# Layer 0 of a four-layer image stack in strips of 16 rows: q and k in one pass with a gathered block transform, v in a second pass

## The chip, the core and the metric

The kernel runs on one core of one Trainium2 chip. A core has TensorE (PE in the profile: matrix products, with PEld for its weight loads), VectorE (DVE), ScalarE (ACT), GpSimd (POOL) and SyncE (SP), which issues DMAs; ACT and POOL issue DMAs too. The five work from queues of their own, each in order, and wait for each other by semaphores. Products go to PSUM (8 banks of 2 KB in each of 128 partitions)[...]. All data are 32-bit floats; a product of such data is issued as two instructions. The metric is the device time of one execution in microseconds (us), the median of several runs.

## What is computed

The input x is (4, 48, 256, 256): 4 images of 48 channels. Four layers follow each other, each of the form x = x + f(groupnorm(x)) with 16 groups. Layer 0, which the change rewrites:

```python
hidden = conv1x1(gn(x), w_hidden) + b_hidden            # 48 -> 288 channels
qkv = depthwise3x3(hidden, w_dw, padding='SAME') + b_dw  # per channel
q, k, v = split(qkv, 3)                                  # 96 channels each
out = irfft2(rfft2(q in 8x8 blocks) * rfft2(k in 8x8 blocks))
normed = (out - mean_c) / sqrt(var_c + 1e-5) * gamma + beta   # over the 96 channels
x = x + conv1x1(v * normed, w_out) + b_out               # 96 -> 48 channels
```

Layers 1 and 2 go the other way about: a 1x1 product to 288 channels, each 8x8 block transformed, multiplied by a mask and transformed back, then a depthwise 3x3 product, gelu of one half times the other half, and a 1x1 product to 48. Layer 3 is a gate from block maxima and variances. Only the order of some steps of layers 1 and 2 is touched, and layer 3 not at all.

## The kernel before

Layer 0 (`layer0`, L227) works in bands of 8 rows, 32 per image, 128 in all. Positions lie on the partitions after the first product. In three steps that are staggered by one band each (the loop at L429):

- `conv_step` (L262) loads 10 rows of x, normalises them (L284), and makes shifted copies with DMAs on SP (L288 to L292), so that the 1x1 and the 3x3 products are a single product: its weights are the products of both (L248, L251). For each half row of 128 positions 4 products of 288 columns add up in PSUM: one of 58 rows (L308) and three of 128 rows (L315). ACT copies q and k out (L320), DVE v (L321).
- `attend_step` (L324) takes four half rows at a time: three products of 384 columns with transform matrices (L335), DVE's two products (L343), two products back (L353), and then mean and variance over the channels (L364 to L374; the power -0.5 is on POOL), scale, gamma, beta on POOL (L375 to L380), and times v on DVE (L381).
- `out_step` (L384) turns the result with products by the unit matrix (L392), multiplies by the output weights (L405), adds x (L407), takes statistics for the next layer (L192) and stores.

The statistics of x itself, for the normalisation of layer 0, come from `stats_step` (L256): all rows of image 0 before its first band, those of image b+1 beside the bands of image b.

Layers 1 and 2 (`layers12`, L442) work in strips of 16 rows, 16 per image, 64 per layer. For strip n, positions of a 8x8 block lie on 64 partitions, for 288 channels in three thirds m: `forward` (L522: normalise, L531; turn, L544; transform, L556), `mix` (L566: 1x1 product, L578, and the mask on DVE, L583), `inverse` (L590: transform back, L604, and ACT's and DVE's copies into z, L612), then halo copies of neighbouring positions within z by DMA, three on SP (L616 to L618) and three on POOL (L619 to L621, the last stores what the strip below needs). `gate` (L628) does the depthwise product: for each channel a 100x64 matrix of taps (built by `build_taps`, L494) times the 64 blocks of z (L640), gelu on ACT (L647), product on DVE (L648). `project` (L671) turns (L655, L658), multiplies (L682) and adds to `res` (L687). `store` (L693) takes the statistics of the 8 rows of `res` (L699) and stores them (L703); `load_res` (L663, L669) then loads the next residual. `bottom` (L707) does the last row of an image. The loop at L752 sets the order: inverse(n,0), gate(n-1,2), mix(n,1), finish(n-1), inverse(n,1), mix(n,2), gate(n,0), forward(n+1), inverse(n,2), mix(n+1,0), gate(n,1).

The functions give the order of the work only roughly: a scheduler sorts the instructions of each engine by when it expects their operands, so an instruction can stand ahead of another that the text has first. Tiles come from pools with a number of buffers; a new tile waits for the last reader of the tile whose buffer it gets. PSUM has 8 tiles of one bank in layer 0 and 4 tiles of two banks in layers 1 and 2.

Of the kernel before, what the change touches and what calls it, by code (L numbers as in the profile page):

```python
# [10 lines left out]
F32 = mybir.dt.float32  # L11
AF = mybir.ActivationFunctionType
ALU = mybir.AluOpType
# [58 lines left out]
def _fft_matrices():  # L72

    rows, real = _frequencies()  # L80
    pr, pc = np.divmod(np.arange(P * P), P)
    names = ("fq", "fr", "fi", "g1", "g2")
    m = {k: np.zeros((128, 128), np.float64) for k in names}
    for row, ((ky, kx), imag) in enumerate(rows):
        angle = 2 * np.pi * ((ky * pr + kx * pc) % P) / P
        cos, sin = np.cos(angle), np.sin(angle)
        weight = (1.0 if (ky, kx) in real else 2.0) / (P * P)
        own = (ky, kx) in real
        for h in (0, 64):
            at = slice(h, h + 64)  # L90
            m["fr"][at, h + row] = cos
            m["fi"][at, h + row] = 0.0 if own else -sin
            m["fq"][at, h + row] = -sin if imag else cos
            m["g1"][h + row, at] = -weight * sin if imag else weight * cos
            m["g2"][h + row, at] = -weight * cos if imag else (0.0 if own else -weight * sin)
    order = np.array([P * r + c for r, c in _order()])
    gz = m["g1"][:, np.concatenate([order, 64 + order])]
    return np.stack([m[k] for k in names] + [gz], 1).astype(np.float32)
# [36 lines left out]
def _ones_rows():  # L135

    padded = np.pad(np.ones((W, W), np.float32), 1)
    out = np.ones((3, 10, P, W), np.float32)
    for n, h0 in enumerate((0, P, W - P)):
        for t in range(9):  # L140
            dy, dx = divmod(t, 3)
            out[n, t] = padded[h0 + dy : h0 + dy + P, dx : dx + W]
    return out
# [16 lines left out]
def conv_stack_kernel(ctx: ExitStack, tc: tile.TileContext, t: dict):  # L160
# [24 lines left out]
    def new_stats(pool, key, bufs):  # L185
        tag = f"stats_{key.rstrip('0123456789')}"
        return pool.tile([C, W // 2, 6], F32, tag=tag, name=f"stats_{key}", bufs=bufs)

    def add_stats(stats, row, rows):

        for n in range(0, rows.shape[1], 2):
            nc.vector.bn_stats(stats[:, (row + n) // 2, :], rows[:, n : n + 2, :])  # L192

# [19 lines left out]
    def over_block(v):  # L213

        return v.rearrange("p (r j c) -> p r j c", r=1, c=1).to_broadcast([C, P, 16, P])

# [10 lines left out]
    def layer0():  # L227
        with ExitStack() as st:
            wp = st.enter_context(tc.tile_pool(name="l0w", bufs=1))
            sb = st.enter_context(tc.tile_pool(name="l0", bufs=2))  # L230
            psum = st.enter_context(tc.tile_pool(name="l0ps", bufs=8, space=PSUM))

            def weight(name, shape):
                dst = wp.tile(shape, F32, tag=name, name=name)
                nc.scalar.dma_start(dst, t[name])
                return dst
# [3 lines left out]
            wh1, w1 = weight("l0_wh1", [128, C6]), weight("l0_wd1", [128, 3, C6])  # L240

            wh2 = wp.tile([122, C6], F32, tag="l0_wh2", name="l0_wh2")
            w2 = wp.tile([122, C6], F32, tag="l0_wd2", name="l0_wd2")
            for p0 in (0, 64):
                nc.scalar.dma_start(wh2[p0 : p0 + 58], t["l0_wh2"])
                nc.scalar.dma_start(w2[p0 : p0 + 58], t["l0_wd2"])
            for k in range(3):
                nc.vector.tensor_tensor(w1[:, k, :], w1[:, k, :], wh1, ALU.mult)  # L248
            for p0 in (0, 64):
                at = slice(p0, p0 + 58)  # L250
                nc.vector.tensor_tensor(w2[at], w2[at], wh2[at], ALU.mult)  # L251
            fft = weight("fft", [128, 6, 128])
            gamma, beta = weight("l0_gamma", [128, C2]), weight("l0_beta", [128, C2])
            w_out, b_out = weight("l0_w_out", [C2, C]), weight("l0_b_out", [C, 1])

            def stats_step(b, band, stats):  # L256
                for row in range(band * P, band * P + P, 4):
                    xt = sb.tile([C, 4, W], F32, tag="xstat", name=f"xstat_{b}_{row}")
                    nc.scalar.dma_start(xt, x_in[b, :, row : row + 4, :])
                    add_stats(stats, row, xt)  # L260

            def conv_step(b, band, mean, rstd):  # L262

                key = f"{b}_{band}"
                lo, hi = max(band * P - 1, 0), min(band * P + P + 1, W)
                at = lo - (band * P - 1)
                n = hi - lo
                xt = sb.tile([C, P + 2, W], F32, tag="x0", name=f"x0_{key}", bufs=4)
                nc.sync.dma_start(xt[:, at : at + n, :], x_in[b, :, lo:hi, :])
                k1 = sb.tile([128, P + 2, W + 2], F32, tag="k1", name=f"k1_{key}")  # L270

                k2 = sb.tile([122, P // 2, W], F32, tag="k2", name=f"k2_{key}")
                kind = 0 if band == 0 else 2 if band == NBAND - 1 else 1
                for i in range(2):
                    nc.sync.dma_start(
                        k2[64 * i + 48 : 64 * i + 58], t["ones"][kind, :, 4 * i : 4 * i + 4]
                    )
                nc.gpsimd.memset(k1[:C, :, 0:1], 0.0)
                nc.gpsimd.memset(k1[:C, :, W + 1 : W + 2], 0.0)
                if band == 0:  # L280
                    nc.gpsimd.memset(k1[:C, 0, :], 0.0)
                if band == NBAND - 1:
                    nc.gpsimd.memset(k1[:C, P + 1, :], 0.0)
                nc.vector.tensor_scalar(  # L284
                    k1[:C, at : at + n, 1 : W + 1], xt[:, at : at + n, :], mean[:C], rstd[:C],
                    ALU.subtract, ALU.mult,
                )
                nc.sync.dma_start(k1[48:96, 0:P, :], k1[0:48, 1 : P + 1, :])  # L288
                nc.sync.dma_start(k1[96:128, 0:P, :], k1[0:32, 2 : P + 2, :])
                for k in range(3):  # L290
                    for i in range(2):
                        nc.sync.dma_start(  # L292
                            k2[64 * i + 16 * k : 64 * i + 16 * k + 16],
                            k1[32:48, 2 + 4 * i : 6 + 4 * i, k : k + W],
                        )
                qk = sb.tile([128, 2 * P, 2 * C2], F32, tag="qk", name=f"qk_{key}")
                v = sb.tile([128, 2 * P, C2], F32, tag="v", name=f"v_{key}", bufs=3)
                for r in range(P // 2):


                    gs = [(i, h) for h in range(2) for i in range(2)]
                    ps = {
                        (i, h): psum.tile([128, 512], F32, tag="ps", name=f"qkv_ps_{key}_{r}_{i}_{h}")
                        for i, h in gs
                    }
                    for i, h in gs:
                        at = slice(64 * i, 64 * i + 58)
                        nc.tensor.matmul(  # L308
                            ps[i, h][:, :C6], k2[at, r, 128 * h : 128 * h + 128], w2[at],
                            start=True, stop=False,  # L310
                        )
                    for i, h in gs:
                        row, w0 = r + 4 * i, 128 * h
                        for k in range(3):
                            nc.tensor.matmul(  # L315
                                ps[i, h][:, :C6], k1[:, row, w0 + k : w0 + k + 128], w1[:, k, :],
                                start=False, stop=(k == 2),
                            )
                        g = 2 * row + h
                        nc.scalar.copy(qk[:, g, :], ps[i, h][:, : 2 * C2])  # L320
                        nc.vector.tensor_copy(v[:, g, :], ps[i, h][:, 2 * C2 : C6])  # L321
                return xt, qk, v

            def attend_step(b, band, qk, v):  # L324

                key = f"{b}_{band}"
                o = sb.tile([128, 2 * P, C2], F32, tag="o", name=f"o_{key}")

                def products(s):
                    f = [  # L330
                        psum.tile([128, 512], F32, tag="ps", name=f"f_{key}_{s}_{n}")[:, : 4 * C2]
                        for n in range(3)
                    ]
                    for n, c0 in enumerate((0, C2, C2)):
# [637 lines left out]
```

## Time and profile before

| | us |
|---|---|
| median of 3 runs | 17339.73 |
| lowest and highest | 17327.48, 17381.77 |
| the profiled execution: its time | 17300.25 |
| its span, first to last instruction | 17298.5 |
| layer 0 (0 to the last product of its last band) | 6802 |
| layers 1 and 2 (to 16252) | 9446 |
| layer 3 | 1047 |

The page lists busy time by engine, then the span in 40 slices (a digit is the busy share in tenths; PEclk is the clock that was granted to TensorE), DMA queues, the chain that ended last, and groups of instructions by line: count, busy time, mean time of one, the idle time before them and what ended it. Busy time of a group counts overlapping instructions once, so busy time by count can be less than the mean of one. In the answers by order of time each line has its start, its length, engine, line, operation, output and inputs, shapes and count, and in brackets the idle time before it and what ended it. The chain that ended last covers only the end of layer 3 here, so it doesn't help for layer 0.

### The profile page before, as it was taken

What the parts mean: (1) busy time and instruction counts of PE and PEld (TensorE: products, weight loads), DVE (VectorE), ACT (ScalarE), POOL (GpSimd) and SP (SyncE); (2) the same over time, 40 slices, a digit from 0 to 9 for tenths busy, and PEclk for the clock granted to TensorE, in tenths of its full rate; (3) what the DMA queues carried; (4) which work ended last, traced back from release to release, by engine and by line L of the source; (5) the groups of instructions that cost most, each with busy time, mean ns of one, the idle gap of its engine ahead of it and who ended that gap; (6) DMA issues with size and microseconds to landing.
All of it is one profiled execution on the core that took longest, in us unless ns stands there. A gap on an engine that the chain in (4) does not pass through costs nothing. (4 is left out here: it accounts for less than half of the span.)

```text
span 17298.5 us, 384653 instructions
## 1 busy us (share of the span) xinstructions
PE 14947.9 (86%) x170196; PEld 10981.8 (63%) x170196; DVE 8709.8 (50%) x13299; ACT 5013.2 (29%) x7570; POOL 3388.3 (20%) x3280
## 2 busy tenths in 40 slices
PE   5999899989989998999999999999999999999400
PEld 3566566656656665777777777777777777777400
DVE  6544544444444444554554545545545545455576
ACT  1222122222222222333333333333333333333222
POOL 0222222222222222111111111111111111111245
PEclk9999999999999998998998989989989989899655
DMA  4222222222222221433433333423433433343467
GB/s 99 58 43 40 63 41 42 40 38 41 43 39 39 41 43 31 87 84 79 86 84 78 84 77 83 87 62 85 88 75 83 88 77 84 79 86 83 84 139 167
DMA packets 276304, 1231.56 MB, mean 71 GB/s; under 512 B 96507, under 2 KB 146757, under 8 KB 163797
## 3 DMA queue, kind: packets, MB, share of 16 engines
q1 hardware_dynamic: 153120, 651.58, 19.1%
q0 software_dynamic: 94720, 452.75, 11.8%
q10 hardware_dynamic: 26804, 102.62, 2.3%
q8 instruction: 1345, 22.04, 0.5%
q14 instruction: 315, 2.57, 0.1%
HBM read 528.04 MB, written 281.54 MB: 47 GB/s over the span
## 5 line engine op out<-in xcount | busy, mean ns | idle before, releaser
L315 PE MATMUL qkv_ps<-l_wd,k 128*128 128x288 f32 x12288 | 3131.2, 412 | 0.0
L315 PEld LDWEIGHTS qkv_ps<-l_wd,k 128*128 128x128 f32 x12288 | 2300.0, 190 | 797.3 <-issue 202.1
L640 PE MATMUL c_ps_False<-z,d 100*64 100x64 f32 x73728 | 2550.1, 235 | 274.8 <-DVE z L612 96.4
L640 PEld LDWEIGHTS c_ps_False<-z,d 100*64 100x64 f32 x73728 | 2497.3, 152 | 423.9 <-DVE z L612 223.4
L612 DVE COPY z<-z_ps 64x1024 f32<-64x1024 f32 x1152 | 1349.0, 1223 | 1387.9 <-ACT z L612 1372.9
L578 PE MATMUL y_ps<-w_in,f 48*128 48x96 f32 x24576 | 1748.8, 298 | 194.2 <-DVE z L612 183.5
L578 PEld LDWEIGHTS y_ps<-w_in,f 48*128 48x128 f32 x24576 | 1617.0, 207 | 471.2 <-DVE z L612 243.8
L647 ACT ACTIVATE g<-c_ps_False 128x512 f32<-128x512 f32 x1152 | 687.9, 597 | 3329.7 <-PE c_ps_False L640 3327.7
L320 ACT COPY qk<-qkv_ps 128x192 f32<-128x192 f32 x2048 | 647.3, 318 | 3327.9 <-PE qkv_ps L315 3045.0
L583 DVE TENSOR_TENSOR yf<-y_ps,mask 128x384 f32<-128x384 f32 x3072 | 1464.6, 547 | 38.5 <-PE y_ps L578 30.0
L648 DVE TENSOR_TENSOR g<-g,c_ps_False 128x512 f32<-128x512 f32 x1152 | 788.4, 687 | 1296.5 <-ACT g L647 1285.3
L658 ACT COPY gt<-gt_ps 72x1024 f32<-72x1024 f32 x1024 | 970.7, 1030 | 1008.8 <-PE gt_ps L655 1008.8
L612 ACT COPY z<-z_ps 64x1024 f32<-64x1024 f32 x1152 | 1087.5, 1008 | 580.7 <-PE z_ps L604 563.0
L321 DVE COPY v<-qkv_ps 128x96 f32<-128x96 f32 x2048 | 473.1, 249 | 1319.9 <-ACT qk L320 1319.8
L604 PE MATMUL z_ps<-yf,dft 64*64 64x512 f32 x9216 | 1120.4, 611 | 7.9 <-DVE yf L583 4.1
L687 DVE TENSOR_TENSOR res<-xo_ps,res 112x1024 f32<-112x1024 f32 x256 | 313.8, 1226 | 1550.9 <-PE xo_ps L682 1544.9
L335 PE MATMUL f<-qk,fft 128*128 128x384 f32 x3072 | 1069.7, 491 | 17.9 <-DVE v L321 17.9
L655 PEld LDWEIGHTS gt_ps<-ident,g 128*72 128x72 f32 x8192 | 904.0, 161 | 127.2 <-issue 111.6
L655 PE MATMUL gt_ps<-ident,g 128*72 128x128 f32 x8192 | 962.1, 276 | 8.6 <-issue 6.6
L682 PE MATMUL xo_ps<-gt,w_out 72*64 72x512 f32 x4096 | 935.4, 598 | 0.0
L619 POOL DMA_DIRECT2D z<-z x384 | 200.9, 523 | 3715.7 <-DVE z L612 3713.7
L343 DVE TENSOR_TENSOR pr<-fq,f 128x384 f32<-128x384 f32 x1024 | 562.6, 553 | 690.9 <-PE f L335 672.0
(135 smaller groups left out, 16261.8 us busy)
## 6 DMA issues: line engine op xcount, KB each, us to landing
z<-z SPq DMA_DIRECT2D x1152, 203.9 KB
xf<-x POOLq DMA_DIRECT2D x256, 384.0 KB, 7.7
x<-x SPq DMA_DIRECT2D x256, 384.0 KB
res<-x POOLq DMA_DIRECT2D x248, 384.0 KB, 6.0
x<-res POOLq DMA_DIRECT2D x248, 384.0 KB, 5.0
carry<-z POOLq DMA_DIRECT2D x384, 204.0 KB, 9.1
z<-carry SPq DMA_DIRECT2D x384, 203.9 KB
x<-in_x SPq DMA_DIRECT2D x120, 480.0 KB
```

What stands on the lines that cost most here:

```text
L315: nc.tensor.matmul(ps[i, h][:, :C6], k1[:, row, w0 + k : w0 + k + 128], w1[:, k, :], start=False, stop=(k == 2),)
L335: nc.tensor.matmul(f[n], fft[:, n, :], qk[:, 4 * s : 4 * s + 4, c0 : c0 + C2], start=True, stop=True,)
L578: nc.tensor.matmul(ps[:, i, 96 * j : 96 * j + 96], f[at, 4 * h + j, :], third(w_in)[at], start=True, stop=True,)
L583: nc.vector.tensor_tensor(y[:, :, 8 * h + i : 8 * h + 8 : 2].rearrange("p (v c) j -> p v c j", v=2), ps[:, i, 0:384].rearrange("p (j v c) ...
L604: nc.tensor.matmul(ps[64 * v : 64 * v + 64, p0 // 64, :], dft[p0 : p0 + 64, 1, p0 : p0 + 64], y[p0 : p0 + 64, c0 : c0 + 16, :].rearrange(" ...
L612: copy[v](z[0:64, :, c0 : c0 + 16, 1 : NP + 1], ps[64 * v : 64 * v + 64].rearrange("p u (c j) -> p u c j", j=NP),)
L640: nc.tensor.matmul(ps[p0 : p0 + 64, v, f0 : f0 + nj], d[rows, HID * v + 48 * m + c, :], z[rows, us, 48 * v + c, 1 : NP + 1], start=True, s ...
L647: nc.scalar.activation(to, of[:, 0], AF.Gelu)
L648: nc.vector.tensor_tensor(to, to, of[:, 1], ALU.mult)
L655: nc.tensor.transpose(ps[:72, k // 4, 128 * (k % 4) : 128 * (k % 4) + 128], g[:, :, j + k], ident)
L658: nc.scalar.copy(gt.rearrange("p q u o -> p (q u o)"), ps[:72].rearrange("p k f -> p (k f)"))
L682: nc.tensor.matmul(ps[64 * i : 64 * i + 64, k, :], w_out[:, p, :], gts[k][i][:, :, p, :], start=(p == 0), stop=(p == 1),)
```

## The change

Layer 0 is rewritten on the pattern of layers 1 and 2, in two passes over all images. Both use `conv_pass` (L277 of the changed kernel), which works in 64 strips of 16 rows and one step for the last rows of all images. A tile z holds one third (96 channels) of hidden: partitions are 64 positions of a patch of 4 rows and 16 columns, then the halo and a row of ones for the bias; free are 4 patch rows, 96 channels, 16 patch columns and two of padding.

- `mixed(n)`: loads and normalises 16 rows, does the 1x1 product for each third with 49 rows (48 channels and a row of ones) and 96 columns, copies into z with ACT and DVE, and fills the halo: on SP three loads of what the strip above stored, and three copies within z; on POOL two copies within z and one store for the strip below.
- `depthwise(n)`: for each channel a 109x64 matrix of taps times 64 columns of z, 32 products to a PSUM tile of two banks, copied by ACT.
- Pass A has thirds q and k. `attend` gathers the 8x8 blocks from their four patches in the transform: for every quarter of the partitions (32 rows) four products add up, of 94 rows of output (64 frequencies and 30 sums of real and imaginary parts) and 384 columns whose elements lie 4 floats apart. ACT copies q's, DVE multiplies by k's in place (three products in place of four per complex frequency), one product of 94 rows goes back, and then the normalisation over channels on tiles twice as wide. The result goes to DRAM (`kept`).
- Pass B has v. `times_v` places it in the same order with products of 32 rows and 64 columns of weights, and multiplies the loaded result by it; `project`, one strip later, turns, multiplies by the output weights, adds x, takes statistics row by row and stores.
- Statistics of x (`stats_rows`) take two rows of both image halves at a time in three tiles.
- In layers 1 and 2 the statistics leave `store` for `add_stats`, which with `load_res` makes `settle`; `gate(n,0)` and then `settle(n-1)` come ahead of `mix(n,2)`.

The diff, cut to its core (constants, weights, and the removed functions of layer 0 are left out):

```diff
+        def conv_pass(name, c_first, thirds, coefs_of, after):
...
+            nz = 2
+            zs = [wp.tile([128, 4, 96, BW], F32, tag=f"z{i}", name=f"z_{name}_{i}") for i in range(nz)]
...
+            def above(zf, n, third):
...
+                lender = lambda src, u: (
+                    nc.sync.dma_start(zf[ABOVE, u, here], src[:, here]),
+                    nc.sync.dma_start(zf[ABOVE_L, u, here], src[15:32:16, to_left]),
+                    nc.sync.dma_start(zf[ABOVE_R, u, here], src[0:32:16, to_right]),
+                )
...
+            def mixed(n):
...
+                for third in range(thirds):
...
+                    above(zf, n, third)
+                    if b is None:
+                        continue
+                    c0 = c_first + 96 * third
+                    for g in range(4):
+                        ps = ps2(f"h_ps_{key(n)}_{third}_{g}")
+                        for j in range(4):
+                            for h in range(2):
+                                at = slice(64 * h, 64 * h + C + 1)
+                                nc.tensor.matmul(
+                                    ps[:, h, 96 * j : 96 * j + 96],
+                                    xn[at, 4 * g + j].rearrange("p r c -> p (r c)"),
+                                    w1[at, c0 : c0 + 96], start=True, stop=True,
+                                )
...
+                    nc.sync.dma_start(zf[ON_LEFT, :, here], zf[COL15, :, to_left])
+                    nc.sync.dma_start(zf[ON_RIGHT, :, here], zf[COL0, :, to_right])
+                    nc.sync.dma_start(zf[ABOVE, 1:4, here], zf[ROWS23, 0:3, here])
+                    nc.gpsimd.dma_start(zf[ABOVE_L, 1:4, here], zf[RIGHT23, 0:3, to_left])
+                    nc.gpsimd.dma_start(zf[ABOVE_R, 1:4, here], zf[LEFT23, 0:3, to_right])
+                    to = lowest[b] if s == S - 1 else carry[(n + 1) % 2]
+                    nc.gpsimd.dma_start(to[:, third, :], zf[ROWS23, 3, :])
...
+            def depthwise(n, zt):
...
+                                nc.tensor.matmul(
+                                    ps[64 * h : 64 * h + 64, k // 8, 64 * (k % 8) : 64 * (k % 8) + 64],
+                                    d[:, 96 * third + c, :], z[0:K, :, c, 1 : NJ + 1],
+                                    start=True, stop=True,
+                                )
+                        nc.scalar.copy(
+                            to[:, 16 * q : 16 * q + 16, :].rearrange("p c j -> p (c j)"),
+                            ps.rearrange("p k f -> p (k f)"),
+                        )
...
+            for n in range(N + after.lag):
+                if n < N:
+                    zt[n] = mixed(n)
+                    if n + 1 < N:
+                        load(n + 1)
+                    after.beside(n)
+                if n >= 1 and n - 1 in convolved:
+                    after.first(n - 1, convolved.pop(n - 1))
+                if after.lag > 1 and 2 <= n:
+                    after.second(n - 2)
+                if n < N:
+                    convolved[n] = depthwise(n, zt.pop(n))
...
+        def by_patch(n, what, s, ch, put):
+            for j in range(4):
+                for h, p, at in quarters:
+                    v = s[at, 24 * ch : 24 * ch + 24, :].rearrange("p c (u j) -> p c u j", j=4)
+                    put(j, h, p, at, v[:, :, :, j])
...
+            def attend(n, convolved):
...
+                    def put(j, h, p, at, moving):
+                        nc.tensor.matmul(
+                            ps[h][0:94, p, 0:384], forward[at, r, j, :], moving,
+                            start=(j == 0), stop=(j == 3),
+                        )
...
+                for ch in range(2):
+                    fs = queries(ch)
+                    keys(ch, fs)
+                    inverse(ch, fs)
...
+                nc.gpsimd.tensor_tensor(var, var, half, ALU.pow)
+                nc.gpsimd.tensor_tensor(o, o, over(var), ALU.mult)
...
+                nc.gpsimd.tensor_tensor(o, o, by_c(gamma), ALU.mult)
+                nc.gpsimd.tensor_tensor(o, o, by_c(beta), ALU.add)
+                nc.sync.dma_start(kept[n], o)
...
+            def times_v(n, convolved):
+                w = sb.tile([128, 2, C2, 16], F32, tag="w", name=f"w_{n}", bufs=3)
+                nc.sync.dma_start(w, kept[n])
...
+                            nc.tensor.matmul(
+                                ps[h][64 * r : 64 * r + 64, p, 0:384], place[at, r, j, :], moving,
+                                start=(j == 0), stop=(j == 3),
+                            )
...
         def store(n):
             layer, b, s = steps[n]
-            if s == 0:
-                stats[0] = wp.tile([HC, P * S, 6], F32, tag="stats_b", name=f"stats_{key(n)}")
-            for r in range(P):
-
-                nc.vector.bn_stats(stats[0][:, P * s + r, :], res[:, r, :])
...
+        def settle(n):
+            add_stats(n)
             if n + 1 < len(steps):
                 load_res(n + 1)
...
             inverse(n, 1)
+            gate(n, 0)
+            if late and s > 0:
+                settle(n - 1)
             mix(n, 2)
-            gate(n, 0)
```

## The prediction

> **What bounds the kernel now.** I read the page's busy shares and slices first, then the busy times by stage, then TensorE's order of time in one band of layer 0 and in one strip of layers 1 and 2.
>
> ```profile
> PE 14947.9 (86%) x170196; PEld 10981.8 (63%) x170196; DVE 8709.8 (50%) x13299; ACT 5013.2 (29%) x7570; POOL 3388.3 (20%) x3280
> ...
> PE   5999899989989998999999999999999999999400
> ...
> PEclk9999999999999998998998989989989989899655
> ```
>
> ```profile
> 0.00:6806.00 6806.00, 6207.64 (x24604) 3951.61 (x24604) 3242.42 (x5810) 1471.08 (x3457) 1711.70 (x922) 0.98 0.23 46
> 6806.00:16252.00 9446.00, 8725.76 (x145576) 7027.64 (x145576) 4682.66 (x7092) 3291.43 (x3977) 1161.93 (x2237) 0.90 0.38 81
> ```
>
> Columns of the second: stretch, length, busy PE, weight loads, DVE, ACT, POOL, granted clock, DMA share, GB/s. Layer 0 takes 6806 us with PE busy 91%, layers 1 and 2 take 9446 us with 92%, but at a clock of 0.90. Both are TensorE's.
>
> ```profile
> 6551.27 1.24 PE L308 MATMUL qkv_ps<-l_wd,k 58*128 58x288 f32 x8
> 6552.44 6.09 PE L315 MATMUL qkv_ps<-l_wd,k 128*128 128x288 f32 x24
> ...
> 6579.93 4.03 PE L335 MATMUL f<-qk,fft 128*128 128x384 f32 x12
> ...
> 6600.59 1.24 PE L308 MATMUL qkv_ps<-l_wd,k 58*128 58x288 f32 x8
> ```
>
> One band costs 49.3 us (6600.59 - 6551.27), almost all of it products that follow each other. A full-array instruction of 384 columns costs 322 ns (12 from 6579.93 to the next group at 6583.80).
>
> ```profile
> 10046.63 2.71 DVE L699 BATCH_NORM_STATS2 stats<-res 112x6 f32<-112x256 f32 x8
> ...
> 10050.65 4.93 PE L578 MATMUL y_ps<-w_in,f 48*128 48x96 f32 x48 [1.53 <-DVE z L612]
> ...
> 10055.51 8.51 PE L640 MATMUL c_ps_False<-z,d 100*64 100x64 f32 x192
> ```
>
> ```profile
> 10048.00:10052.00 4.00, 2.47 (x38) 2.31 (x34) 3.97 (x8) 1.24 (x2) 0.47 (x1) 0.91 0.79 188
> 10052.00:10056.00 4.00, 4.00 (x44) 3.83 (x43) 3.97 (x8) 0.00 (x0) 2.11 (x5) 0.50 0.89 174
> ```
>
> A strip of layers 1 and 2 takes 68.2 us. The statistics on DVE hold up its z copies, PE waits 1.53 us, and then its clock is halved for about 10 us: L578 takes 103 ns an instruction instead of 61, L640 8.5 us instead of 5.82. The same drop stands 68 us later, and again around 12040, 12108, 14020 and 14088.
>
> **What the skill says.** "TensorEngine Tiling (Array Packing)", Tiling Modes: products of at most 32 rows can run as four row tiles at once. "TensorE: Matmul & The Clock Gate", Part 3, gives 3.07x as measured for four row tiles at 512 columns. The trace agrees for 2x2 tiles: L604, 64 rows by 64 columns, costs 117 ns for 512 columns (24 in 2.81 us), against 322 x 512/384 = 429 ns for a full array, 3.7x. The same page, Part 1, has the halved clock after idle; here 1.5 us of idle sufficed. "SBUF — State Buffer", Door 1: The DMA port swizzle, says that SBUF is read in lines of 16 bytes and that each access to a new line pays a penalty. No row of before shows a moving operand of that kind.
>
> **The change, pass A (q and k), per strip of 16 rows, full clock.**
> - 1x1 product: 64 matmuls = 128 instructions. L578 has their form (64 in 3.9 us, 61 ns): 7.8 us. Their evacuation (8 copies of 768 columns each on ACT, 0.80 as L548, and on DVE, 0.95 by L612's slope) keeps pace.
> - Depthwise: 192 matmuls = 384 instructions like L640 (192 in 5.82): 11.7 us.
> - Gathering DFT: 128 matmuls = 256 instructions, 32 rows, 384 columns. Four at once would be 322/4 = 81 ns, by the page's 3.07 it is 105, two at once 161. Their moving operand steps 4 floats, a new line each time. I take 95: 24.3 us.
> - Inverse: 32 instructions of 384 columns in two column tiles, 171 ns (L682's 228 x 384/512): 5.5 us. Twice PE waits about 1 us for DVE's last product: 2 us.
> - Sum on PE: 51.3 us. ACT (25 us) and DVE (32 us, with 2x L364, L366 and L372) lie under it.
>
> But a second chain decides. From the end of one strip's inverse: evacuation 0.8, mean 3.5, subtract 3.5, squares and sums 5 make 13 us. Then POOL: power 5.4 (2x L374's 2.93, rounded down for its fixed part), times rstd 5.5, gamma and beta 6.9 each (2x L375, L379, L380), 24.7. The store of this o stands on SP ahead of the next strip's halo copies, and POOL's own halo copies stand behind the POOL work. What must then move: 1.57 MB of o and 0.79 MB of x at 238 GB/s (188 at share 0.79), 2.4 MB of halo at 165 (99 at share 0.60, 10012 to 10016): 24 us, and 2 to land. So the second third of the depthwise two attends later can't begin before T+64. Behind it follow 5.8 + 7.8 + 31.8 to the end of that attend: two periods = 109.4, one 54.7. PE then waits about 3.4 us in a strip, which by the drop above costs another 5 us of halved clock on this chain: 57 us. Without the wait 50, with DMA and POOL half as slow again 65.
> 65 x 57 = 3705.
>
> **Pass B (v), per strip.** 1x1 3.9; depthwise 5.8; placing 128 instructions of 32x64 tiles: 42 ns with eight at once, 85 with four; I take 55, 7.0 us; 64 transposing instructions at 130 ns (L392: 8 in 1.04), 8.3; output product 16 at 228, 3.7. Sum 28.7. DVE has 17 us, ACT 10, POOL 5. DMA has 5.4 MB, 24 us at the rates above, with slack of some 17 us in each strip because o is loaded a strip ahead. For bubbles and a halved clock I add 4.3 (the 4.9 us drop of before in most strips): 33. Range 29.5 to 38. 65 x 33 = 2145.
>
> **Once.** Statistics of image 0: before, 165 us with two tiles in flight; three now: 110. Depthwise matrices 128 instructions, 41 us (L502's 61.7 x 192/288). The statistics of images 1 to 3 stand in DVE's queue within the first few strips, 330 us against 5 x 57: 60 more. Zeroing for the last rows 30, end of A and start of B 110, two strips' tail of B 40. Sum 390.
>
> Layer 0: 3705 + 2145 + 390 = 6240 against 6806: -566.
>
> **Layers 1 and 2.** In the changed kernel's order on DVE the statistics lie between the z copies (5, copy, 2, copy, 1, copy), and on PE the 192 depthwise instructions follow the inverse directly, the mask product after them. Each z copy is then in time: the 1.53 us wait and the 4.9 us of halved clock go. What is late next is xn: it stands on DVE behind the 8 mask products, and the cover it had on PE (the 5.85 us of L640) now lies ahead. PE ends the mask product at +12.5 us from the inverse's start, xn's first half is ready at +15.2: a new wait of 2.7 us, ahead of products as thin as those where the clock fell. From inverse to end of forward: 26.4 us before; 23.0 with no drop, 27.6 if the clock falls there (L544 and L556 at the slow rate, +4.6). I take -1.1 us, near the middle; the ends are -3.4 and +1.2. Times 120 strips: -130 (-410 to +145). On POOL's queue the res load moves behind that strip's three halo issues (0.5 us each), which no longer wait with it for the store to land (3.6 us before 10051.53); its data is wanted 40 us later, so I cost this at nothing; without that cover it would be its 6.0 us to landing.
>
> **Sum.** 17298 - 566 - 130 = 16602 us of span; outside the span lie 1.8 us (17300.25), and the median of the runs is 39 above that: **16640**.
>
> **Rivals.**
> 1. *Row tiles don't overlap by four, or the 16-byte step halves the read (slower; 0.20).* At 161 ns the DFT takes 41.2 us: PE 68.2 us per strip, which hides the POOL chain. Pass A +11.2 x 65 = 730; placing at 85 ns, +250. 17,620. It decides from about 150 ns an instruction, where 700 us are gone. For it: no such product in the trace; against: L604's 3.7x.
> 2. *No stall and no drop (faster, 0.13).* A 50, B 29.5, layers 1 and 2 at -3.4: -455 - 230 - 280, 15,680. For it: the depthwise rows recover; against: 1.5 us sufficed for a drop.
> 3. *The POOL and SP chain is half as slow again (0.17).* A 65, B 35: +520 + 130: 17,290, about the old time, of which a fifth lies slower than 0.3% and a fifth within.
> The likeliest case, 0.50, has 16,200 to 17,050.
>
> **Chances.** A measurement of this kernel tells 0.3%, some 50 us. Slower: 0.19 of rival 1 and 0.03 of rival 3, 0.22; within: 0.01 and 0.04, 0.05; faster 0.73. The range 15,900 to 17,550 leaves out a good half of rival 1 and of rival 2, 0.2 in all.
>
> **What would show it.** Period of pass A near 57 us with PE waiting for a halo DMA between the two thirds of the depthwise; DFT instructions at 80 to 105 ns (150 or more is rival 1); period of pass B near 33; in layers 1 and 2 no wait at the mask product behind z copies but one at xp for xn, and a strip of 65 to 69.5 us. Wrong it would be if DVE or ACT lines ended PE's longest waits in either pass, or if the first strips took over 400 us.

## The result, and the profile after

| | before | after |
|---|---|---|
| median of 4 runs | 17,354.97 us | 18,428.32 us |
| ratio, 95% interval | | 1.062 (1.0599 to 1.0641) |
| profiled execution, span | 17,298.5 us | 18,418.5 us |
| layer 0 | 6806 us | 7570 us |
| layers 1 and 2 | 9446 us | 9805 us |

The change is slower, by 6.2%, where I had forecast 4% faster. Both halves of the forecast failed: layer 0 lost 764 us instead of gaining 566, and layers 1 and 2 lost 359 instead of gaining 130.

The page of the changed kernel gives busy times, TensorE (PE) in 40 slices, and the clock granted to it.

```profile
PE 15806.6 (86%) x225764; PEld 11181.0 (61%) x225764; DVE 9257.5 (50%) x10792; ACT 5900.6 (32%) x6669; POOL 4020.5 (22%) x3765
...
PE   5999999999979999899898998999989989989600
...
PEclk8889999989989999888888998997989888889755
```

The same by stage: pass A, pass B, layers 1 and 2 (columns as in the prediction).

```profile
136.00:5325.00 5189.00, 4835.32 (x51619) 2627.46 (x51622) 2676.80 (x1738) 1632.00 (x1798) 1881.01 (x769) 0.89 0.31 73
5461.00:7570.00 2109.00, 1951.93 (x28018) 1257.02 (x28017) 1028.39 (x1421) 695.43 (x711) 363.84 (x581) 0.95 0.73 163
7570.00:17375.00 9805.00, 8890.29 (x145586) 7214.75 (x145586) 4676.30 (x7111) 3296.37 (x3977) 1169.60 (x2248) 0.88 0.37 78
```

PE is busy 93% of pass A: for the most part it isn't waiting, its work takes longer than I gave it. The pass takes 5189 us against 3705; pass B takes 2109 against 2145. One strip of pass A, PE in order of time:

```profile
2799.92 11.05 PE L487 MATMUL qf<-s_qk,l_fft 32*94 32x384 f32 x64
2810.78 11.01 PE L487 MATMUL kf<-s_qk,l_fft 32*94 32x384 f32 x64
2821.72 0.86 PE L514 MATMUL o_ps<-qf,l_fft 94*64 94x384 f32 x2
...
2825.53 11.41 PE L400 MATMUL c_ps_qk<-z_qk,d_qk 109*64 109x64 f32 x380
2836.87 1.14 PE L368 MATMUL h_ps_qk<-l_w,xn_qk 49*128 49x96 f32 x16
2839.69 12.24 PE L368 MATMUL h_ps_qk<-l_w,xn_qk 49*128 49x96 f32 x112 [1.69 <-ACT s_qk L405]
```

64 instructions of the DFT take 10.86 us (2810.78 - 2799.92): 170 ns each, where I took 95 and gave 161 as the worst. The 1x1 product (L368) waits 1.69 us for ACT and then needs 109 ns an instruction (12.24 / 112) instead of 61. Both engines around that wait, another strip:

```profile
3064.58 3.36 DVE L534 TENSOR_TENSOR o<-o,mu 128x3072 f32<-128x3072 f32 x1
...
3068.03 2.86 ACT L538 ACTIVATE sq<-o 128x1536 f32<-128x1536 f32 x2 [3.53 <-DVE o L534]
...
3070.80 2.82 ACT L405 COPY s_qk<-c_ps_qk 128x1024 f32<-128x1024 f32 x3
...
3071.84 6.51 PE L368 MATMUL h_ps_qk<-l_w,xn_qk 49*128 49x96 f32 x58 [1.70 <-ACT s_qk L405]
```

ACT's squares stand ahead of the last three copies of the depthwise result and wait for DVE's subtraction. The copies come late, and with them the PSUM tiles that the 1x1 product needs. Behind the wait the granted clock is 0.50 from 3072 to 3088.

In pass B, turning (L631) and placing (L593):

```profile
6505.70 1.99 PE L631 MATMUL t_ps<-ident,w 128*96 128x128 f32 x16
...
6524.12 11.06 PE L593 MATMUL v_ps<-s_v,l_fft 32*64 32x384 f32 x128
```

Placing takes 86 ns an instruction, where I took 55. In layers 1 and 2, from one `inverse` to the end of the next `forward`:

```profile
12022.16 2.81 PE L835 MATMUL z_ps<-yf,dft 64*64 64x512 f32 x24
12024.90 5.82 PE L871 MATMUL c_ps_False<-z,d 100*64 100x64 f32 x192
12030.65 3.81 PE L809 MATMUL y_ps<-w_in,f 48*128 48x96 f32 x64
12037.19 0.40 PE L775 MATMUL xp_ps<-ident,xn 48*64 48x48 f32 x4 [2.73 <-DVE xn L762]
12038.48 6.92 PE L775 MATMUL xp_ps<-ident,xn 48*64 48x48 f32 x124 [0.89 <-DVE xn L762]
12045.33 5.54 PE L787 MATMUL f_ps<-dft,xp 128*128 128x128 f32 x32
```

The wait behind the z copies at L809 is gone, the forecast wait for xn is there with 2.73 us (2.7 forecast), and the clock falls behind it, to 0.50 from 12039 to 12048: L787 takes 171 ns an instruction (12050.80 - 12045.33 for 32), against 117 in k4 below, which has no wait there. The stretch takes 28.6 us (26.4 before). Other strips are alike: from 8000 to 16000 us the products on xn (L775) take 302 ns on the mean, against 227 before (L544), and PE waits 368 us for xn, about 3.5 us a strip.

### The profile page after: what moved, and what is told of

It is laid out like the page before. It is cut to its first block, busy times and chain, and to the rows that moved or that the text cites. A ratio compares the mean times of both kernels' runs of the same rounds, so it can differ in the third digit from the quotient of the medians.

```text
span 18418.5 us, 494130 instructions
## 1 busy us (share of the span) xinstructions
PE 15806.6 (86%) x225764; PEld 11181.0 (61%) x225764; DVE 9257.5 (50%) x10792; ACT 5900.6 (32%) x6669; POOL 4020.5 (22%) x3765
## 5 line engine op out<-in xcount | busy, mean ns | idle before, releaser
L871 PEld LDWEIGHTS c_ps_False<-z,d 100*64 100x64 f32 x73728 | 2292.2, 142 | 495.0 <-DVE z L843 246.1
L809 PE MATMUL y_ps<-w_in,f 48*128 48x96 f32 x24576 | 1512.5, 276 | 5.2 <-issue 4.5
L809 PEld LDWEIGHTS y_ps<-w_in,f 48*128 48x128 f32 x24576 | 1425.0, 188 | 150.4 <-ACT z L843 103.1
L487 PE MATMUL kf<-s_qk,l_fft 32*94 32x384 f32 x8320 | 1483.8, 850 | 33.0 <-ACT qf L500 33.0
L487 PE MATMUL qf<-s_qk,l_fft 32*94 32x384 f32 x8320 | 1489.9, 855 | 11.0 <-ACT s_qk L405 6.2
L507 DVE TENSOR_TENSOR qf<-qf,kf 94x768 f32<-94x768 f32 x520 | 473.7, 946 | 1970.0 <-PE kf L487 1966.3
L775 PE MATMUL xp_ps<-ident,xn 48*64 48x48 f32 x16384 | 964.4, 302 | 446.5 <-DVE xn L762 446.5
L775 PEld LDWEIGHTS xp_ps<-ident,xn 48*64 48x64 f32 x16384 | 929.7, 215 | 482.3 <-issue 363.3
L487 PEld LDWEIGHTS kf<-s_qk,l_fft 32*94 32x94 f32 x8320 | 489.6, 177 | 983.7 <-issue 917.5
L542 POOL TENSOR_TENSOR var<-var,neg_half 128x32 f32<-128x32 f32 x65 | 354.4, 5453 | 3206.1 <-DVE var L540 3206.1
L487 PEld LDWEIGHTS qf<-s_qk,l_fft 32*94 32x94 f32 x8320 | 463.5, 190 | 893.6 <-issue 838.3
## 6 DMA issues: line engine op xcount, KB each, us to landing
xf<-x POOLq DMA_DIRECT2D x256, 384.0 KB, 11.4
```

What stands on the lines that cost most here:

```text
L487: nc.tensor.matmul(ps[h][0:94, p, 0:384], forward[at, r, j, :], moving, start=(j == 0), stop=(j == 3),)
L507: nc.vector.tensor_tensor(f[:, h], f[:, h], ps[0:94, :, 0:384], ALU.mult)
L775: nc.tensor.matmul(ps[p0 : p0 + 64, j // 8, 64 * (j % 8) : 64 * (j % 8) + C], xn[at, 16 * h + j].rearrange("p r c -> p (r c)"), ident[at, ...
L809: nc.tensor.matmul(ps[:, i, 96 * j : 96 * j + 96], f[at, 4 * h + j, :], third(w_in)[at], start=True, stop=True,)
L871: nc.tensor.matmul(ps[p0 : p0 + 64, v, f0 : f0 + nj], d[rows, HID * v + 48 * m + c, :], z[rows, us, 48 * v + c, 1 : NP + 1], start=True, s ...
```

## The experiments

Theory after the result: (1) the DFT and the placing run at half rate because their moving operand steps 4 floats, while four row tiles do overlap; (2) layers 1 and 2 lose by the wait for xn and the halved clock behind it; (3) pass A loses some 7 us a strip because ACT's squares stand ahead of its copies. Main rival of (1): only two row tiles overlap, whatever the layout. The chips of the later runs were up to 0.5% slower (before: 17,417 to 17,446 us), so kernels are compared by their ratio to before on the same chip.

| kernel | ratio to before (95%) | strip of A | pass A | pass B | layers 1, 2 |
|---|---|---|---|---|---|
| changed kernel | 1.062 (1.0599 to 1.0641) | 78.9 | 5237 | 2087 | 9659 |
| k1_contiguous | 1.0109 (1.0092 to 1.0127) | 64.3 | 4426 | 2108 | 9643 |
| k2_read_only | 1.0104 (1.0089 to 1.0119) | | 4422 | 2112 | 9657 |
| k3_order_before | 1.0455 (1.043 to 1.0481) | | 5238 | 2076 | 9464 |
| k4_xn_ahead | 1.0144 (1.0106 to 1.0182) | | 5235 | 2089 | 8991 |
| k5_raw_squares | 1.0516 (1.0494 to 1.0537) | 77.1 | 5132 | 2106 | 9652 |
| k7_contig_squares | 0.9935 (0.9918 to 0.9951) | 60.0 | 4119 | 2103 | 9640 |
| k8_contig_halo_sp | 0.989 (0.9874 to 0.9906) | 58.1 | 4000 | 2118 | 9693 |
| k6_all | 0.9491 (0.9469 to 0.9513) | 60.0 | 4103 | 2101 | 8881 |
| k11_best | 0.9324 (0.9297 to 0.9351) | 56.4 | 3934 | 1986 | 8866 |
| k9_before_new_order | 1.0126 (1.0102 to 1.0149) | | | | 9641 |
| k12_before_again | 0.998 (one run) | | | | 9405 |
| k10_steps | 1.030 (one run) | 70.4 | | | |

Stages in us: pass A from its first 1x1 product to the last inverse, pass B from its first 1x1 product to the last placing, layers 1 and 2 from the first product on xn to the last output product. These cuts leave out set-up and ends, so they differ from the windows above. A strip of A is the mean over the 1800 us from 2000 to 3800; the number of strips in them is that of the DFT instructions divided by 256 (changed kernel: 5842, so 22.8 strips).

**k1_contiguous** and **k2_read_only.**

```diff
-    to[:, 16*q : 16*q+16, :].rearrange("p c j -> p (c j)"), ps.rearrange("p k f -> p (k f)")
+    to[:, 16*q : 16*q+16, :].rearrange("p c (j u) -> p c j u", j=4),
+    ps.rearrange("p k (c u j) -> p (k c) j u", c=8, j=4)
...
-    v = s[at, 24*ch : 24*ch+24, :].rearrange("p c (u j) -> p c u j", j=4); put(..., v[:, :, :, j])
+    v = s[at, 24*ch : 24*ch+24, :].rearrange("p c (j u) -> p c j u", j=4); put(..., v[:, :, j, :])
```

k2 has only the second half of it.

> ACT's copies of the depthwise result now store the four column phases apart (order c, j, u in place of c, u, j), so that the DFT and the placing read runs of 16 neighbouring floats; nothing else changes. Theory (the moving operand's step of 4 floats halves the read, four row tiles do overlap): DFT falls from 170 ns an instruction to 85 to 105, placing from 86 to 43 to 55; pass A from 77 us a strip to about 58, pass B from 31.9 to about 28, total about 16,950 us (16,750 to 17,150). Rival (only two of the four row tiles overlap, whatever the layout): 170 and 86 ns stay, total 18,430 within 60.

> Only the reading side of the edit before: DFT and placing read runs of 16 neighbouring floats, but ACT's copies store them as in the changed kernel, so the DFT mixes up the positions of a block (this part of the computation is altered). It tells TensorE's read from ACT's permuted copy. Theory: DFT and placing as in the kernel with both sides, total within 60 us of that. Rival (the permuted copy on ACT is dearer than the 1.02 us of the straight one and takes part of the gain): this one is faster by more than 60 us. Second rival (two row tiles only): 170 ns and 18,430.

k1, all engines in order of time, from ACT's squares to the next depthwise:

```profile
2513.77 2.86 ACT L538 ACTIVATE sq<-o 128x1536 f32<-128x1536 f32 x2
2515.28 5.59 DVE L539 TENSOR_REDUCE var<-sq 128x16 f32<-128x1536 f32 x2 [6.32 <-ACT sq L538]
...
2521.18 5.45 POOL L542 TENSOR_TENSOR var<-var,neg_half 128x32 f32<-128x32 f32 x1 [35.16 <-DVE var L540]
...
2526.71 6.67 POOL L543 TENSOR_TENSOR o<-o,var 128x3072 f32<-128x3072 f32 x1
2527.47 6.99 DVE L344 TENSOR_SCALAR xn_qk<-x_qk,mean_l,rstd_l 48x2048 f32<-48x2048 f32 x1
...
2533.46 6.29 POOL L545 TENSOR_TENSOR o<-o,l_gamma 128x3072 f32<-128x3072 f32 x1
2534.39 0.99 DVE L375 COPY z_qk<-h_ps_qk 64x768 f32<-64x768 f32 x1
2535.41 5.42 DVE L344 TENSOR_SCALAR xn_qk<-x_qk,mean_l,rstd_l 48x2048 f32<-48x2048 f32 x1
...
2535.43 4.79 PE L487 MATMUL qf<-s_qk,l_fft 32*94 32x384 f32 x26 [5.87 <-DVE z_qk L375]
...
2539.83 6.29 POOL L546 TENSOR_TENSOR o<-o,l_beta 128x3072 f32<-128x3072 f32 x1
...
2546.06 0.66 POOL L384 DMA_DIRECT2D z_qk<-z_qk  x1
...
2549.38 5.42 PE L487 MATMUL qf<-s_qk,l_fft 32*94 32x384 f32 x64
...
2554.61 5.34 PE L487 MATMUL kf<-s_qk,l_fft 32*94 32x384 f32 x64
...
2558.42 1.72 SPq L383 DMA_DIRECT2D z_qk<-z_qk  x1
...
2570.32 1.98 PE L400 MATMUL c_ps_qk<-z_qk,d_qk 109*64 109x64 f32 x32 [6.46 <-DMA z_qk<-z_qk]
```

At full clock the DFT takes 82 ns an instruction (64 in 5.23 us from 2549.38). A full array needed 322 ns for the same columns before, so the four row tiles overlap 3.9 times: theory (1) holds, the rival falls. k2's median agrees within 3 us, so the permuted copy on ACT costs nothing that shows. But the ratio is 1.0109, not the 0.977 of the expectation (16,950 / 17,355), for two reasons. Pass B didn't move, though placing fell from 86 to 48 ns (128 instructions in 6.19 us): its depthwise now waits for halo copies, 283 us in all instead of 20. In k1:

```profile
5717.81 7.79 PE L400 MATMUL c_ps_v<-z_v,d_v 109*64 109x64 f32 x192 [5.36 <-DMA z_v<-z_v]
...
5729.28 6.27 PE L593 MATMUL v_ps<-s_v,l_fft 32*64 32x384 f32 x128
5735.47 1.99 PE L631 MATMUL t_ps<-ident,w 128*96 128x128 f32 x16
```

And a strip of pass A takes 64.3 us, not 58: PE waits 6.5 us for halo copies and 5.9 us for DVE, and both follow POOL. POOL works from 2521 to 2546 on o; only then are the halo copies issued, on POOL itself, and on SP behind the store of o. This is the second chain of the prediction, at 64 us instead of 57.

**k7_contig_squares** and **k8_contig_halo_sp**, each on top of k1. In the diff the first part, up to var, is k7 (the squares now come ahead of the subtraction of the mean), the rest k8 (halo stands for POOL in three copies).

```diff
+    for r in range(2): nc.scalar.activation(sqs[r], o[:, r], AF.Square)
...
+    nc.vector.tensor_tensor(mu2, mu, mu, ALU.mult)
+    nc.vector.tensor_tensor(var, var, mu2, ALU.subtract)
...
+    halo = nc.sync if name == "qk" else nc.gpsimd
-    nc.sync.dma_start(kept[n], o)
+    nc.gpsimd.dma_start(kept[n], o)
```

> Both edits, runs of 16 neighbouring floats for the DFT and the unreduced squares. Theory (with the fast DFT a strip of pass A is a loop: halo lands, half of the depthwise, three copies on ACT, squares behind them, sums, 25 us of POOL, halo issued behind POOL, halo lands; the squares were ready for it 9.7 us earlier): a strip falls from 65.5 us to 56 to 58, the 57 us of the prediction's chain, total some 550 us below the kernel with the contiguous reads alone, ratio 0.978 (0.972 to 0.986). Rival (the halo copies or DVE's order are late for reasons of their own): strip 63 or more, ratio 1.00 or more.

> Runs of 16 neighbouring floats for the DFT, and in pass A all halo copies on SP and the store of o on POOL, so that no halo copy stands behind POOL's work on o. Theory (the 5 to 6.5 us that PE waits for halo copies in each strip of the kernel with contiguous reads come from POOL's 25 us ahead of them): the wait and the halved clock behind it go, strip from 65.5 to 56 to 58, ratio 0.978 (0.972 to 0.988). Rival (issuing and moving the halo on one queue is itself the limit): wait for a halo DMA stays, strip 63 or more, ratio 1.00 or more.

k8, PE:

```profile
2521.22 11.39 PE L401 MATMUL c_ps_qk<-z_qk,d_qk 109*64 109x64 f32 x380
...
2535.37 3.34 PE L369 MATMUL h_ps_qk<-l_w,xn_qk 49*128 49x96 f32 x48 [1.70 <-ACT s_qk L406]
2539.95 7.14 PE L369 MATMUL h_ps_qk<-l_w,xn_qk 49*128 49x96 f32 x64 [1.24 <-DVE z_qk L376]
...
2578.67 1.51 PE L401 MATMUL c_ps_qk<-z_qk,d_qk 109*64 109x64 f32 x45
```

Depthwise follows depthwise at 57.45 us, with no wait for a halo: 363 us of them in k1, none here. So the wait came from POOL's work, and the store of its result on SP, ahead of the halo issue, as the prediction had it. What sets the period now is PE's own work with the waits of the 1x1 product, for ACT (109 us in all, as in the changed kernel) and for DVE, and the halved clock behind them. k7 shortens the same chain from the other end (the squares no longer wait behind copies that wait for the halo): 60.0 us, short of the 56 to 58 expected; 270 us of halo waits are left. Its totals, and k8's, miss the expected ratios by 0.011 to 0.016; the strips account for part, a dearer start of the pass for more: pass A less 65 strips is 224 us in k8, 108 in the changed kernel, with 73 us in k8 where PE waits for the statistics' loads.

**k5_raw_squares**, the squares of k7 on the changed kernel alone.

> The changed kernel, but ACT squares the unreduced result (variance as the mean of the squares minus the square of the mean), so that the squares stand on ACT right behind the copies of the result and wait for nothing on DVE; the six copies of the depthwise result then follow without a stop. Theory (of the changed kernel's 77.6 us a strip of pass A, some 7 are this stop: PE waits 1.7 us at the 1x1 product for ACT's copies, and the halved clock makes its 128 instructions 13.4 us instead of 7.8): strip 70 to 72, total about 450 us below the changed kernel, ratio to the kernel before 1.036 (1.030 to 1.042). Rival (DVE's mean, subtraction and sums are as late as ACT was, so z copies make PE wait at the same place and the clock falls as before): 1.055 or more.

The ratio, 1.0516, lies between the two ranges, nearer to the rival's: 1.8 us a strip, not 7. PE, k5:

```profile
2574.18 3.82 PE L368 MATMUL h_ps_qk<-l_w,xn_qk 49*128 49x96 f32 x64
2579.94 0.35 PE L368 MATMUL h_ps_qk<-l_w,xn_qk 49*128 49x96 f32 x2 [1.94 <-DVE z_qk L375]
```

ACT's wait is gone (109 us in k3, whose pass A is that of the changed kernel, 12 here), and DVE's z copies, behind mean, sums and subtraction, are as late (25 us, now 117). The wait moved; theory (3) named one of two. That the wait, not the product, makes it slow is shown by k7, where the same 128 instructions follow without one: 7.39 us.

**k3_order_before, k9_before_new_order, k12_before_again, k4_xn_ahead.** k3 takes the order of layers 1 and 2 back, k9 puts it into the kernel before. k4 keeps it, but normalises earlier and elsewhere:

```diff
+    normal[n] = [sb.tile([HC, 16, P, P], F32, tag="w4", ..., bufs=4) for h in range(2)]
...
     inverse(n, 1)
+    if ahead: normalise(n + 1)
     gate(n, 0)
```

> The changed kernel with layers 1 and 2 in the order of the kernel before (mask product ahead of the depthwise of the first third, statistics and residual load with the store). Theory (the loss of 359 us in layers 1 and 2 is the new order's own wait for xn and the halved clock behind it): layers 1 and 2 back to about 9,446 us from 9,805, layer 0 as it was, total 18,070 (18,020 to 18,120). Rival (the clock of layers 1 and 2 fell for a reason that lies outside them, such as the longer layer 0): 9,805 stays, total 18,430.

> The kernel before with one thing of the change alone: the new order in layers 1 and 2 (depthwise of the first third ahead of the mask product of the last, statistics and residual load later). Theory (the order costs by itself what taking it back saved in the changed kernel, 195 us between the traces and 288 between the medians): ratio 1.0165 (1.010 to 1.018). First rival (the whole 340 us by which layers 1 and 2 of the changed kernel exceed those of before is the order): 1.0195 or more. Second rival (the order costs nothing, layers 1 and 2 suffer from the new layer 0): within 0.3% of before.

> The kernel before once more, to read its stages on the same chip as the other kernels of this call. Theory (the 145 us by which layers 1 and 2 of the changed kernel with the old order exceed those of before in the first trace are the chip and its granted clock): from the first product on xp to the last output product of layers 1 and 2 9,319 us in the first trace, 9,360 to 9,470 here. Rival (they come from the new layer 0): 9,300 to 9,350.

> The changed kernel, but the next strip's xn is normalised ahead of the depthwise of the first third, into two buffers of its own instead of the one that the mask product still reads. Theory (the 2.7 us wait at xp and the halved clock behind it are the whole loss, and the wait at the z copies stays away): a strip of layers 1 and 2 falls from 70.8 us to 64.5 to 66.5, layers 1 and 2 to about 9,050 us (8,980 to 9,300), total about 17,680 (17,600 to 17,930). Rival (another wait, of DVE's z copies or of ACT's copy of xp, takes its place and keeps the clock down): layers 1 and 2 at 9,450 or more, total 18,070 or more.

Taking the order back saves 195 us between traces (9659 to 9464), about half of the 359 expected, and 288 by the ratios (1.062 to 1.0455). Putting it in costs 236 between traces (9405 to 9641) and 216 between medians (17,417 to 17,633). So the order by itself costs some 200 to 290 us, not 359. The first trace of before has 9319 us in this stretch, the second 9405: 86 us are the difference between two runs of one kernel. Of the 340 us between the first two traces (9319 to 9659) these leave 254, within that range. k4 takes the wait away, PE:

```profile
12066.95 4.23 PE L877 MATMUL c_ps_False<-z,d 100*64 100x64 f32 x128 [0.32 <-DVE z L849]
12071.12 3.81 PE L815 MATMUL y_ps<-w_in,f 48*128 48x96 f32 x64
12074.86 3.93 PE L781 MATMUL xp_ps<-ident,xn 48*64 48x48 f32 x128
12078.73 3.84 PE L793 MATMUL f_ps<-dft,xp 128*128 128x128 f32 x32
```

The stretch from inverse (12061.82) to the end of forward (12082.49) takes 20.7 us instead of 28.6, and layers 1 and 2 take 668 us less: theory (2) holds. The new order with xn ahead beats the old order as it was by 414 us (against k12); the old order with xn ahead was not run.

**k10_steps**: the DFT's step, q at every 2nd float, k at every 8th.

```diff
+    c = 24*ch + 12*(j // 2)
+    if what == "qf": v = s[at, c : c+12, :].rearrange("p c (u j) -> p c u j", j=2); put(..., v[:, :, :, j % 2])
+    elif what == "kf": v = s[at, 0:48, :].rearrange("p c (u j) -> p c u j", j=8); put(..., v[:, :, :, 4*ch + j])
```

> The changed kernel with two other steps of the DFT's moving operand: the products on q read every second float, those on k every eighth (both then take other positions and channels than the DFT needs, so this part of the computation is altered; the number and size of the products stay). Known: step 1 in runs of 16 takes 82 ns an instruction, step 4 takes 170. First theory (each 16-byte line that is touched costs one access, a line of 4 floats and a line of 1 cost the same): step 8 takes 170 as step 4 does, and step 2 lies at or below 126, the half-way. Second theory (cost grows with the distance passed over): step 8 about 340, step 2 about 82. Third (any step that isn't 1 halves the read): 170 for both.

```profile
2716.11 5.65 PE L495 MATMUL qf<-s_qk,l_fft 32*94 32x384 f32 x64
2721.59 11.21 PE L495 MATMUL kf<-s_qk,l_fft 32*94 32x384 f32 x64
2732.73 0.86 PE L522 MATMUL o_ps<-qf,l_fft 94*64 94x384 f32 x2
```

Step 2 takes 86 ns (64 in 5.48 us), step 8 takes 174 ns, as step 4 does. This is the first theory, with lines of 16 bytes (4 floats): two reads from each line go at nearly the full rate, one goes at half, and passing over more lines adds next to nothing. A step of 3 was not run.

**k6_all** (k1, k5, k4) and **k11_best** (also k8, and in pass B the depthwise one strip later):

```diff
+    wait = after.lag - 1
+    for n in range(N + after.lag + wait):
...
+        m = n - wait
...
+        if m in zt: convolved[m] = depthwise(m, zt.pop(m))
```

> Contiguous reads, unreduced squares and xn ahead in layers 1 and 2 together. If the three act on different places their gains add: the kernel with the first two minus the some 670 us that xn ahead took from layers 1 and 2, ratio 0.937 (0.928 to 0.948), faster than both kernels. Rival (the time saved in layer 0 is given back in layers 1 and 2 through a lower granted clock): layers 1 and 2 over 9,200 us, ratio 0.955 or more.

> All that has helped together: contiguous reads, unreduced squares, halo copies of pass A on SP and the store of o on POOL, xn ahead in layers 1 and 2; and one thing more, in pass B the depthwise of a strip follows the 1x1 product of the next one, so that its halo copies have a whole strip's time to land. Theory (pass B with contiguous reads stays at 32.4 us a strip because PE waits 5 to 6 us for halo copies that were issued 16 us earlier, a latency and not the DMA's throughput): pass B falls to 26.5 to 28.5 us a strip, pass A to 55 to 60 on the mean, ratio to the kernel before 0.917 (0.908 to 0.930). Rival (the DMA engines, busy 0.74 of pass B, are themselves the limit): pass B stays at 31 or more, ratio 0.933 or more.

The gains of layer 0 and of layers 1 and 2 add: k6 is 781 us below k7, and layers 1 and 2 didn't slow down. (Its ratio misses the expected range by 0.001; that of k7, on which it builds, misses by more.) k11 is the fastest, 6.8% under the kernel before and 12% under the changed one. In pass B its halo wait is gone, yet a strip takes 30.6 us, not 28. PE, k11:

```profile
5013.12 4.84 PE L401 MATMUL c_ps_v<-z_v,d_v 109*64 109x64 f32 x160
5022.41 1.98 PE L401 MATMUL c_ps_v<-z_v,d_v 109*64 109x64 f32 x32 [4.45 <-issue]
5024.32 7.15 PE L369 MATMUL h_ps_v<-l_w,xn_v 49*128 49x96 f32 x64
```

PE stops for 4.45 us in the middle of a group, waiting for nothing that the profile shows ("issue", 140 us at this line), and the clock halves. Neither the expectation nor its rival (31 or more) held; what PE waits for there is open. It is at a time of many transfers (share 0.77, 173 GB/s), which is no proof.

## Why the prediction was wrong, step by step

- **Gathering DFT: "I take 95".** The step that failed. It measured 170 ns, 19.2 us more in a strip. That lifts PE's sum from 51.3 to 70.5 us, 13.5 above the chain's 57 on which the forecast rested: some 880 of the 1484 us by which pass A missed. The prediction named the step of 4 floats and then gave it no price in this term; it took a value between full overlap (81) and the 3.07 of "TensorE: Matmul & The Clock Gate", Part 3 (105), as if only the overlap were open. The overlap is 3.9 (k1). The Trainium skill, "SBUF — State Buffer", Specifications (TRN2), says that full bandwidth needs at least two hits in each 16-byte line; a step of 4 floats has one. k1, k10 and the changed kernel agree: 82, 86, 170, 174 ns for steps 1, 2, 4, 8.
- **Rival 1** had the right side, and the right cause as the second of its two; its 17,620 us is 810 short. It kept the gain in layers 1 and 2, and it took 161 ns and a 1x1 product at full clock.
- **1x1 product, "their evacuation keeps pace".** Evacuation is the copy out of PSUM. It didn't keep pace: 13.4 us with 1.7 us of wait ahead, not 7.8: 7.3 us a strip, 475 us in the pass. The prediction's sum on PE, 51.3, with 19.2 for the DFT and these 7.3 is 77.8; the trace has 77.7 (L487 begins at 2774.14 and at 2851.86). I had summed ACT's 25 us and DVE's 32 as lying under PE, and not asked what stands in a queue ahead of a copy. On ACT the late copies are those of the depthwise result, which still held PSUM; without that wait DVE's z copies are as late (k5).
- **The second chain, 57 us.** It was hidden: PE had 78 us of work. When k1 made the DFT fast it came out, with the forecast wait for the halo but at 64 us: squares and sums were ready not at T+13 but at T+22 (2499.15 to 2521.09 in k1). Of these 9 us the squares waited 4.8 (2508.97 to 2513.77), because they stand behind copies that wait for the halo. The rest are sizes: the mean took 5.3 us instead of 3.5, squares and sums 7.3 instead of 5. Taking POOL out of the halo's way (k8) removes that wait. That k8's strip of 57.45 us is near the chain's 57 is luck: it is PE's sum with the waits of the 1x1 product.
- **Depthwise** 11.4 (11.7), **inverse** with its waits 6.7 (7.5): right.
- **Pass B, 33**: 32.1, right by luck, because two errors cancel. Placing took 86 ns instead of 55 (+4.0 us). Turning is 32 instructions in a strip (2080 in 65 steps), one for each product by the unit matrix and not two, where the prediction counted 64 (4.2 us instead of 8.3). Bubbles and a clock of 0.95 then take some 3.5 us, of which 2.4 are idle time ((2109 - 1952) / 65), near the forecast 4.3.
- **Once, 390**: 136 to the start of pass A and 136 between the passes; some 108 more at the start of pass A, which the window of pass A holds.
- **Layers 1 and 2, "I take -1.1 us, near the middle".** The first wait was forecast to 0.03 us (2.73); a second one behind it, 0.89 us for the rest of xn, was not. What failed besides is the choice that the clock would fall in about half the strips. The mean of 302 ns on xn's products says that it fell in nearly all, and the stretch cost 28.6 us, above the upper end of 27.6. With the difference between runs of one kernel on top: +359 instead of -130.
- **The sum**, against the prediction's span of 16,602: pass A +1484, pass B -36, once -118 (136 + 136 - 390), layers 1 and 2 +489, together 1819; the span is 1816 above, because layer 3 took 3 us less.

## What to carry over

Before gathering with a step in a moving operand, count the reads in each 16-byte line: a permutation in the copy out of PSUM, which happens anyway, gave the DFT its rate back at no cost that showed. Where a forecast wait stands ahead of products, price it with the halved clock behind it, and look for a buffer that lets the producer run earlier. When the engine that bounds gets faster, the chain that it hid appears; find it by following one strip around until it closes on itself.

## What the hardware showed unexpectedly

xn on DVE (L344, 48x2048) takes 1.34 us in pass B and 5.8 us on the mean in pass A of k1. In the k1 fence each ends 1.0 to 1.1 us after a POOL operation has: at 2534.46 and 2540.83, POOL's at 2533.38 and 2539.75. "SBUF — State Buffer", SBUF: two separate sides, says that DVE, in some of its operations, and GpSimd share a port pair by an exclusive lock and the loser blocks; these rows fit it, but no run here takes POOL away. The z copy behind xn was late by it, and PE waited 5.9 us for that copy in the middle of the DFT.

DVE's reductions lost too. For the same 128x1536 elements L539 takes 2.8 us, where L372 took 1.73 before. The changed layout has them read elements 16 floats apart, where before they lay side by side; no run here tells whether this is the reason.

Behind a wait of 1.70 us the clock was halved for some 16 us (3072 to 3088), behind 1.53 us in the kernel before for some 10 (10051.5 to 10061.5). Not every wait of this size does it: behind one of 1.40 us at L640 in the kernel before (14055.49) the clock stayed at 1.00.
